# Reordering three places of a one-core audio tower kernel: additions of bo in group 0, transposes of x2 in group 1, bias rows in the last group

## The chip, the cores and the metric

One core of one Trainium2 chip. The metric is the device time of one execution in microseconds (us), over several runs; the profile is of one such execution, and its span (first to last instruction) is about 1.8 us shorter than the time. Engines: PE is TensorE's matmuls, PEld its weight loads, DVE VectorE, ACT ScalarE, POOL GpSimd, SP the sync engine. "SPq" and "ACTq" lines are DMA issues. "DMA share" is the mean busy share of the core's 16 DMA engines. "Half clock" means a stretch in which the profile's clock record grants TensorE half its speed; a "window" of it, in the recorded texts, is 3.41 us, the shorter of the two such stretches of the profile before ahead of the tail (the other has 6.83 us).

## The reference, cut to what matters

64 signals of 80,000 samples are cut into 157 frames of 512, put through an orthonormal DCT, and then through one layer:

```python
h = _L0_tok_ref(x)                                     # DCT of frames: (64, 157, 512)
h = h + _L0_attn_ref(_layernorm(h), Wk, bk, Wq, ...)   # phase attention, cumulative sums, gate
h = h + _L0_ffn_ref(_layernorm(h), Wg, bg, We, be)     # one of 16 experts for each signal

# attention, its end:
return x + total / norm @ Wo + bo
# experts:
scores = softmax(mean(x, axis=1) @ Wg + bg); idx = argmax(scores)
y = einsum('bsd,bdo->bso', x, We[idx]) + be[idx][:, None, :]
return gate * y
```

Everything is float32. The expert's matrix We[idx], 1 MB for each signal, and its bias row be[idx] can only be fetched once the router has decided.

## The kernel before: the parts that matter

The kernel works in 16 groups of four signals. A group has five "frames" of 128 tokens: four of the signals' first 128 tokens, and one (index GB = 4) that gathers the four tails of 29. While group g is in attention, group g+1 is embedded and group g-1 is in the experts. The order of the program matters on each engine: in the profile before, GpSimd runs the five additions of bo (from 44.64 us) and only then the layer norm that stands behind them (51.22).

```python
def add_bo(g, m):                     # GpSimd, 128x512
    r = S[g]["res"][m]
    nc.gpsimd.tensor_tensor(r, r, bo, ALU.add)

def phasors(g):                       # ScalarE: eight sines; then GpSimd
    ...
    nc.gpsimd.tensor_copy(by_tail(kf_t[: 2 * F]), kf[: 2 * F, :, P:L])

def turn_x2(g):                       # transposes on TensorE, each copied out by ScalarE
    for m in range(NM):
        place(s["x2T"], m, transposed(s.pop(("x2", m))), copy=copy)
        yield

for g in range(NG):
    turns = turn_x2(g - 1)
    project(g, turns if g > 1 else iter(()))   # from group 2 on, transposes between projections
    phasors(g)
    if behind:
        fold_once(g + 1, 0); fold_once(g + 1, 1); fold_twice(g + 1, 0)
        for m in range(NM):
            value(g, m)
            for _ in turns:                    # group 1: here
                pass
            if m == 0:
                route(g - 1)
                fold_twice(g + 1, 1)
                keep_value(g, m)
                route_sum(g - 1)
            elif m == 1:
                route_spread(g - 1)
            ...
    else:
        ...
        for m in range(NM):
            add_bo(0, m)                       # group 0: five at once
    for m in range(NM):
        ... embed and embed_ln of group g+1, load_frame, add_bo(g + 1, m)
        gate_part(g, m); turn(g + 1, m); scores
```

fold_once is an addition on VectorE and a subtraction on GpSimd, fold_twice two additions on VectorE; keep_value evicts a value on VectorE, that is, moves it out of the tile that TensorE wrote; route_sum reduces the router's result on VectorE and route_spread gives it back to TensorE.

The last group has no successor to hide behind. fetch asks for expert matrices (four buffers), bias for bias rows (four buffers named be, which also hold the result until its output DMA is done), add_bias adds the residual on VectorE, expert does the matmuls, the eviction and the output. The kernel follows whole; its end is the part in question.

## Time and profile before

| | before |
|---|---|
| time, median (lowest to highest) | 1566.69 us (1565.12 to 1566.76, 3 runs) |
| TensorE busy | 1538.3 us, 98% of a span of 1564.9 |
| VectorE, ScalarE, GpSimd busy | 45%, 28%, 34% |
| DMA | 135 MB, 86 GB/s in the mean |

TensorE is the bound, so I read where it stands still and what follows its last matmul. The lines are in the prediction. In the same profile's table by stretches (first column the stretch in us; the value before DMA share and GB/s is the clock granted to TensorE), two stretches show half the clock, one from shortly before the end of its longest stop (53.32) and one 1.8 us after the end of the next (112.61):

```profile
53.00:56.30 3.30, 2.98 (x13) 2.99 (x14) 0.75 (x2) 3.25 (x5) 2.23 (x4) 0.50 0.00 0
114.40:121.20 6.80, 6.13 (x39) 2.91 (x38) 0.66 (x2) 1.87 (x2) 0.72 (x1) 0.50 0.01 2
```

### The profile page before, as it was taken

To read this page: it belongs to the slowest core of one execution; us is meant where nothing else is said; L and a number is where in the kernel's file an instruction comes from. 1 tells how busy PE (TensorE), PEld (TensorE's weight loads), DVE (VectorE), ACT (ScalarE), POOL (GpSimd) and SP (SyncE) were. 2 spreads that over 40 slices of the span, in tenths; PEclk is the share of its full clock that TensorE was granted. 3 is DMA by queue.
4 is the path that set the end of the run, shared out by engine and by line. 5 is a ranking of instruction groups with operands and counts; after the bars stand their busy time and mean duration, and the time that the engine had idled before them with its cause. 6 is when DMAs were issued, how large, how long until landed. Compare 5 with 4: busy or idle time off the path is not lost.

```text
span 1564.9 us, 17536 instructions
## 1 busy us (share of the span) xinstructions
PE 1538.3 (98%) x6242; PEld 891.3 (57%) x6242; DVE 697.9 (45%) x1676; ACT 445.1 (28%) x676; POOL 529.9 (34%) x964
## 2 busy tenths in 40 slices
PE   8889999999999999999999999999999999999997
PEld 5646557465564746647465474655647456474552
DVE  4344544435444444444445443454443544444253
ACT  4332233331323314223142233313233142331210
POOL 3523423243332433323343242432324333233132
PEclk9999999999999999999999999999999999999999
DMA  5103141141311323122231311313113131222216
GB/s 182 34 0 135 41 146 49 48 141 54 137 38 47 142 61 134 34 86 103 67 134 34 133 60 57 142 48 141 41 47 141 61 134 34 72 83 65 110 36 205
DMA packets 42856, 135.26 MB, mean 86 GB/s; under 512 B 7873, under 2 KB 8401, under 8 KB 34193
## 3 DMA queue, kind: packets, MB, share of 16 engines
q0 software_dynamic: 15616, 88.09, 16.6%
q1 hardware_dynamic: 26920, 45.81, 9.0%
q8 instruction: 50, 0.82, 0.2%
q10 hardware_dynamic: 232, 0.24, 0.1%
q14 instruction: 38, 0.30, 0.1%
HBM read 113.53 MB, written 20.58 MB: 86 GB/s over the span
## 4 chain that ended last, share of the span: by engine, by line
PE 95%; DMA 2%; ACT 1%; DVE 1%; POOL 1%; issue 1%; SPq 0%; DVEq 0%; POOLq 0%
PE mm L181 48%; PE mm L401 17%; PE mm L442 9%; PE tr L162 5%; PE mm L198 4%; PE mm L590 3%; PE mm L366 2%; PE mm L196 2%; PE mm L455 2%; PE tr L495 1%; PE tr L416 1%; DMA out<-be 1%; DMA be<-in_be,expi 1%; DMA frame<-in_frames 0%; POOL res L216 0%
## 5 line engine op out<-in xcount | busy, mean ns | idle before, releaser
L401 PE MATMUL mm<-xT,wg 128*128 128x314 f32 x1024 | 281.1, 426 | 0.0
L401 PEld LDWEIGHTS mm<-xT,wg 128*128 128x128 f32 x1024 | 192.5, 188 | 72.0 <-issue 0.5
L181 PE MATMUL mm<-wv,xT 128*128 128x512 f32 x512 | 231.4, 600 | 1.7 <-ACT xT L168 1.7
L181 PE MATMUL mm<-we,x2T 128*128 128x512 f32 x512 | 223.0, 593 | 1.4 <-DMA we<-in_we,rows 1.4
L181 PE MATMUL mm<-wo,tT 128*128 128x512 f32 x512 | 222.3, 592 | 0.0
L474 ACT ACTIVATE x<-res,shift,rstd 128x512 f32<-128x512 f32 x80 | 65.1, 814 | 383.8 <-POOL shift L156 383.8
L181 PEld LDWEIGHTS mm<-we,x2T 128*128 128x128 f32 x512 | 97.0, 190 | 123.8 <-issue 120.9
L181 PEld LDWEIGHTS mm<-wo,tT 128*128 128x128 f32 x512 | 97.3, 190 | 117.2 <-issue 114.8
L153 POOL TENSOR_SCALAR rstd<-mv 128x1 f32<-128x1 f32 x160 | 42.0, 263 | 350.4 <-DVE mv L151 345.5
L181 PEld LDWEIGHTS mm<-wv,xT 128*128 128x128 f32 x512 | 94.1, 191 | 107.2 <-issue 104.5
L208 ACT ACTIVATE x<-mm,shift,rstd 128x512 f32<-128x512 f32 x80 | 62.2, 777 | 309.0 <-POOL shift L156 308.6
L442 PE MATMUL mm<-att,v 128*128 128x314 f32 x512 | 143.2, 427 | 0.0
L471 DVE TENSOR_TENSOR res<-mm,res 128x512 f32<-128x512 f32 x80 | 55.3, 692 | 150.1 <-PE mm L181 150.1
L598 DVE SCALAR_TENSOR_TENSOR be<-mm,gate,be 128x512 f32<-128x512 f32 x80 | 60.0, 751 | 118.3 <-PE mm L181 76.8
L442 PEld LDWEIGHTS mm<-att,v 128*128 128x128 f32 x512 | 94.9, 190 | 31.3
L162 PE MATMUL tr<-ident,x 128*128 128x128 f32 x640 | 94.0, 278 | 10.1 <-ACT x L208 5.1
L162 PEld LDWEIGHTS tr<-ident,x 128*128 128x128 f32 x640 | 74.0, 141 | 52.4 <-ACT x2T L168 17.7
L568 POOL DMA_INDIRECT be<-in_be,expi x80 | 82.7, 1034 | 61.0 <-issue 23.7
L430 DVE TENSOR_TENSOR tT<-mm,gT 128x314 f32<-128x314 f32 x128 | 62.3, 487 | 90.3 <-PE mm L442 84.9
L216 POOL TENSOR_TENSOR res<-res,bo 128x512 f32<-128x512 f32 x80 | 101.7, 1273 | 2.4 <-ACT res L210 2.4
L154 POOL TENSOR_TENSOR rstd<-rstd,power 128x1 f32<-128x1 f32 x160 | 96.1, 601 | 13.4
L388 POOL COPY kf_t<-kf 64x116 f32<-64x116 f32 x16 | 4.4, 278 | 271.2 <-ACT kf L385 271.2
(121 smaller groups left out, 1792.6 us busy)
## 6 DMA issues: line engine op xcount, KB each, us to landing
frame<-in_frames SPq DMA_DIRECT2D x80, 256.0 KB
out<-be SPq DMA_DIRECT2D x64, 256.0 KB
out<-be SPq DMA_DIRECT2D x60, 32.0 KB
out<-be SPq DMA_DIRECT2D x60, 26.0 KB
be<-in_be,expi POOLq DMA_INDIRECT x80
wv<-in_wv SPq DMA_DIRECT2D x1, 1024.0 KB
wg<-in_wg SPq DMA_DIRECT2D x1, 1024.0 KB
wo<-in_wo SPq DMA_DIRECT2D x1, 1024.0 KB
```

Of the source, the lines that this page charges most:

```text
L154: nc.gpsimd.tensor_tensor(rstd, rstd, power, ALU.pow)
L162: nc.tensor.transpose(tr[:, c * P : (c + 1) * P], x[:, c * P : (c + 1) * P], ident)
L181: nc.tensor.matmul(ps, lhs(c), w[:, c, :], start=(c == 0), stop=(c == C - 1))
L198: nc.tensor.matmul(by_r[:, 1::2, :], ft[:, i, :], dct_o[:, i, :], start=(i == 0), stop=(i == 1))
L208: nc.scalar.activation(x, h, AF.Identity, bias=shift, scale=rstd)
L216: nc.gpsimd.tensor_tensor(r, r, bo, ALU.add)
L401: nc.tensor.matmul(ps[:, k, : 2 * L], wg[:, c, o * P : (o + 1) * P], s["xT"][:, c, 2 * k : 2 * k + 2, :L], start=(c == 0), stop=(c == C - 1),)
L430: nc.vector.tensor_tensor(to, reads[0], th, ALU.mult)
L442: nc.tensor.matmul(ps[:, c, : 2 * L], s["v", i][:, cols], att[:, i], start=True, stop=True)
L474: nc.scalar.activation(x, r, AF.Identity, bias=shift, scale=rstd)
L568: nc.gpsimd.indirect_dma_start(out=be, out_offset=None, in_=a["be"], in_offset=bass.IndirectOffsetOnAxis(ap=s["expi"][:, m : m + 1], axis=0),)
L598: nc.vector.scalar_tensor_tensor(o, ps, s["gate"][:, m : m + 1], o, ALU.mult, ALU.add)
```

## The change

The intent: take the two stops of TensorE in the first groups away, and in the last group request bias rows without waiting for outputs to leave the buffers, and evict each frame without first adding the next frame's bias. The diff, without blank lines:

```diff
     def bias(g, m):
         s = S[g]
-        s["be", m] = be = p2.tile([P, D], F32, tag="be", name="be", bufs=4)
+        if g + 1 < NG:
+            be = p2.tile([P, D], F32, tag="be", name="be", bufs=4)
+        else:
+            be = p1.tile([P, C, P], F32, tag="frame", name="be_last", bufs=NM).rearrange("p c t -> p (c t)")
+        s["be", m] = be
...
         project(g, turns if g > 1 else iter(()))
+        if g == 1:
+            value(g, 0)
+            for _ in turns:
+                pass
         phasors(g)
...
             for m in range(NM):
-                value(g, m)
-                for _ in turns:
-                    pass
+                if m > 0 or g > 1:
+                    value(g, m)
...
             fold_twice(1, 4)
-            for m in range(NM):
-                add_bo(0, m)
...
+            if g == 0:
+                add_bo(0, m)
             if ahead:
                 add_bo(g + 1, m)
...
     pick_gate(g)
+    order = [0, 1, 2, GB, 3]
+    bias(g, order[0])
     add_bias(g - 1, ORDER[3])
     add_bias(g - 1, ORDER[4])
     expert(g - 1, ORDER[2])
-    order = [0, 1, 2, GB, 3]
-    bias(g, order[0])
     expert(g - 1, ORDER[3])
     fetch(g, [2])
     bias(g, order[1])
+    bias(g, order[2])
     expert(g - 1, ORDER[4])
     fetch(g, [3])
-    bias(g, order[2])
-    add_bias(g, order[0])
-    add_bias(g, order[1])
+    bias(g, order[3])
+    bias(g, order[4])
     for n, m in enumerate(order):
+        add_bias(g, m)
         expert(g, m)
-        if n + 3 < NM:
-            bias(g, order[n + 3])
-        if n + 2 < NM:
-            add_bias(g, order[n + 2])
```

I call the three places A (bo, group 0), B (transposes of x2, group 1) and C (last group).

## The prediction

> **What bounds the kernel now.** I read the page's busy shares and its chain of work first, then the timeline of TensorE alone to find where it stands still, then the timeline of all engines around each stop, and last DMA share and landing times in the final 40 us.
>
> ```profile
> PE 1538.3 (98%) x6242; PEld 891.3 (57%) x6242; DVE 697.9 (45%) x1676; ACT 445.1 (28%) x676; POOL 529.9 (34%) x964
> PE 95%; DMA 2%; ACT 1%; DVE 1%; POOL 1%; issue 1%; SPq 0%; DVEq 0%; POOLq 0%
> ```
>
> TensorE is busy 98% of the span and 95% of the chain. From the third group on, groups repeat every 95.28 us (values of group 3 start at 305.36, of group 2 at 210.08 in the chain in order of time) with almost no gap, so only stops of TensorE, or the tail after it, can be gained. The change touches three places; I show each.
>
> Place A, group 0, first gate stage (timeline; start, length, then the instruction):
>
> ```profile
> 44.13 4.47 PE L401 MATMUL mm<-xT,wg 128*128 128x314 f32 x16
> 44.64 6.50 POOL L216 TENSOR_TENSOR res<-res,bo 128x512 f32<-128x512 f32 x5
> ...
> 51.22 0.21 POOL L153 TENSOR_SCALAR rstd<-mv 128x1 f32<-128x1 f32 x1
> ...
> 53.32 1.12 PE L162 MATMUL tr<-ident,x 128*128 128x128 f32 x4 [4.71 <-ACT x L208]
> ...
> 57.10 4.39 PE L401 MATMUL mm<-xT,wg 128*128 128x314 f32 x16
> ```
>
> Five additions of bo sit ahead of the layer norm of group 1's first frame in GpSimd's queue; TensorE waits 4.71 us for the normalised x, and works at half speed after it.
>
> Place B, group 1, between value of frame 0 and the router:
>
> ```profile
> 107.91 0.47 ACT L384 ACTIVATE kf<-u 32x314 f32<-32x314 f32 x1
> ...
> 111.99 1.04 ACT L168 COPY x2T<-tr 128x512 f32<-128x512 f32 x2
> ...
> 112.61 1.13 PE L162 MATMUL tr<-ident,x 128*128 128x128 f32 x8 [3.57 <-ACT x2T L168]
> ...
> 115.36 2.32 PE L495 MATMUL tr<-x2T,rwg 128*32 128x157 f32 x32 [0.67 <-ACT x2T L170]
> 117.61 5.46 PE L181 MATMUL mm<-wv,xT 128*128 128x512 f32 x8
> ```
>
> Eight sines on ScalarE are ahead of the copies that empty the two transpose banks. Again a stop, then half speed: the router takes 2.32 us (1.27 at 213.45), value of frame 1 takes 5.46 (3.70 at 214.65).
>
> Place C, the last group:
>
> ```profile
> 1542.31 0.95 POOL L568 DMA_INDIRECT be<-in_be,expi  x1 [8.35 <-DMA out<-be]
> 1543.57 0.94 POOL L536 DMA_INDIRECT we<-in_we,rows  x1 [0.30 <-issue]
> ...
> 1553.06 0.95 POOL L568 DMA_INDIRECT be<-in_be,expi  x1 [5.15 <-DVE be L598]
> ```
> ```profile
> 1549.90 3.62 PE L590 MATMUL mm<-we,x2T 128*32 128x512 f32 x26 [0.77 <-DMA we<-in_we,rows]
> 1553.45 3.70 PE L181 MATMUL mm<-we,x2T 128*128 128x512 f32 x8
> ```
> ```profile
> 1557.58 0.75 DVE L579 SCALAR_TENSOR_TENSOR be<-be,gate,res 128x512 f32<-128x512 f32 x1 [3.82 <-DMA be<-in_be,expi]
> 1558.25 1.41 DVE L598 SCALAR_TENSOR_TENSOR be<-mm,gate,be 128x512 f32<-128x512 f32 x2
> 1559.03 3.60 ACTq L606 DMA_DIRECT2D out<-be  x8
> 1559.68 0.33 SPq L600 DMA_DIRECT2D out<-be  x1
> ```
>
> A bias row waits for an output to leave its buffer; the fourth expert matrix queues behind it on GpSimd. At the end the last bias row comes late, and the tails' eviction stands behind its addition on VectorE, although TensorE finished the tails at about 1553.5. Eight outputs are issued after it, the last at 1562.21; it lands at 1563.8, and the program ends 1.04 us later.
>
> [...] its clock records stand at 0.5 for 3.41 us from 52.9 and 6.83 us from 114.4, exactly after the stops of A and B. [...] additions of line 100 take 1.34 us beside the bo additions, 0.28 elsewhere. [...] an output of 256 KB takes 9.3 us beside expert matrices (1532.28 to 1541.5) and 2.2 us alone at the end.
>
> **The change, part by part.** No arithmetic is added or removed; TensorE's instruction order is identical, and only orders on ScalarE, VectorE and GpSimd, and one buffer, change.
>
> A. The five bo additions become one per step. VectorE: without them lines 100 and 101 run at 0.28, so the first statistics start at about 45.4 rather than 47.49 and end at 46.3; GpSimd's three small steps take 1.23 (51.22 to 52.45), so x is started at 47.7 and written at 48.45. The gate's matmuls end at 44.13 + 4.23 = 48.36. The stop shrinks to about 0.1. From the transposes to the next gate stage takes 2.28 us in group 1 (140.28 to 142.56), so it starts at 50.8 rather than 57.10: **6.2 us**, of which 4.6 is the stop and 1.6 the half clock. Two additions (2 x 1.27) a step plus 1.3 of statistics fit well inside a step of 6.5.
>
> B. Copies before sines. Transposes start at 108.00 as before; in group 2 the first copy starts 0.70 after the transposes, so at 108.7. From first copy to router takes 3.37 now (111.99 to 115.36), so the router starts at about 112.0, 3.3 earlier; with 1.2 for it and 3.53 for value of frame 1 TensorE is through at 116.7 rather than 122.9. But the sines now start late: copies end at 112.0, the table load takes 1.28 and four sines 2.14, so kf is complete at 115.4. In group 2, which already has this order, VectorE's router sum ends 3.25 us after the copy of kf (214.16 to 217.41), since a frame's folding on GpSimd and an eviction stand between. That gives 118.7, so the next TensorE step, spreading that sum, starts 2.0 us late, at about 118.75 against 122.91: **4.1 us**, not 6.2. I subtract 0.3 for a chance of about one in six that sparse transposes or this new stop still halve the clock (about 1.7 us for one window). Say 3.8.
>
> C. With its own buffers no bias row waits for an output. The third matrix still waits for TensorE (issued 1533.02, landed 1544.3 behind 3.25 MB; the 1.43 us stop there stays). The fourth can be requested when TensorE leaves its old buffer, about 1537 rather than 1543.57. DMA share is about 0.9 to 1.0 from 1532 to 1542, so its gain is less than those 6.5: after the third matrix (mostly landed by 1542) come two bias rows, 0.5 MB, and 1 MB; at 2.75 us per MB (landings at 226.5, 230.3, 232.7, 235.6 in group 2) that is 1546.2[...]. The tails' matmuls start at 1548.07; uninterrupted they take 3.64, now they take 5.45. TensorE thus ends about 1.8 earlier at best, 1.2 in the mean, at about 1555.9. Then the last eviction 0.75, issue, 2.16 to landing (1559.68 to 1561.84 now) and 1.04 to the end: 1555.9 + 0.1 + 0.75 + 2.16 + 1.04 = 1559.95. The tails' branch: eviction done by about 1553.2, eight issues 3.6, landing and end 2.2: 1559.0, just behind. Against 1564.9: **5.0 us**.
>
> Sum: 6.2 + 3.8 + 5.0 = 15.0 us, about 1.0%. They add, since they lie one after another on TensorE's chain. 1566.69 - 15.0 = 1551.7.
>
> **Rivals.** First: B only moves the wait. Then the new stop at the router's sum takes most of it, helped by a halved clock: B gives 1 to 2 and the total is about 1554. For it speaks that VectorE and GpSimd have a serial chain from the sines to the sum; against it that even with this chain I count 4. Second: C's matrices are bound by DMA, so the early request gains nothing on TensorE, which ends at 1557.0; only the freed eviction counts: 3.7 for C, total 1553. For it speaks DMA share near 1.0; against it the share of 0.35 in 1542 to 1544, a hole the new order fills. Third: bo additions now collide with VectorE in every step of group 0 and delay the masked scores; the slack of several us a step speaks against it. It would cost A 1 us. Fourth, upward: no half clock at all, and the fourth matrix in time: about 1550.5.
>
> **Range and chances.** A 5.5 to 6.6, B 1.5 to 4.5, C 3.5 to 6.0; runs before spread over 1.6 us[...]. Point 1551.7, range 1549.0 to 1555.5. Over 2% faster would need 31 us, twice all that is here: 1%. Over 2% slower needs an unknown failure: 1%. Within 2%: 98%.
>
> **What would show it.** A: the stop of 4.71 gone, second gate stage of group 0 near 50.8, no half clock there. B: copies ahead of the table load, router near 1.27 us, a new stop of about 2 us before the spread. C: no bias row waiting for an output; the fourth matrix requested near 1537; tails' matmuls in about 3.7 us; the tails' eviction before 1553; the last output from the sync queue last. I am wrong if the clock is still halved in group 1 for two windows, if the third matrix lands later because more requests and outputs share the engines, or if the middle groups' period moves from 95.28.

## The result, and the profile after

1551.22 us in the median (1550.40 to 1551.95, 6 runs) against 1566.03 of the kernel before in the same rounds (1564.23 to 1566.76, 6 runs). The ratio is 0.9906, with a 95% interval from 0.9894 to 0.9919. (A ratio is the mean time of one kernel's fast runs over that of the other's of the same rounds, so not quite the ratio of the medians.)

Busy shares and chain of the changed kernel:

```profile
PE 1534.1 (99%) x6242; PEld 889.2 (57%) x6242; DVE 696.5 (45%) x1676; ACT 445.0 (29%) x676; POOL 527.1 (34%) x964
PE 96%; DMA 1%; issue 1%; POOL 0%; DVE 0%; ACT 0%; SPq 0%; POOLq 0%
```

TensorE's busy time fell by 4.2 us with the same 6242 matmul records: they were not fewer, but fewer of them ran at half clock (10.24 us of it in A and B before, none there after).

Place A, timeline of all engines:

```profile
43.43 4.46 PE L401 MATMUL mm<-xT,wg 128*128 128x314 f32 x16
...
47.73 0.64 PE L162 MATMUL tr<-ident,x 128*128 128x128 f32 x4
...
48.46 2.75 POOL L216 TENSOR_TENSOR res<-res,bo 128x512 f32<-128x512 f32 x2
...
50.05 4.39 PE L401 MATMUL mm<-xT,wg 128*128 128x314 f32 x16
```

The transposes follow the gate without a stop (no bracket), the bo additions come later, two in a step, and the second gate stage starts 6.62 us after the first instead of 12.97.

Place B, the same view:

```profile
101.59 1.07 ACT L168 COPY x2T<-tr 128x512 f32<-128x512 f32 x2 [2.12 <-PE tr L162]
...
104.85 1.28 ACT L384 ACT_TABLE_LOAD   x1
104.89 1.27 PE L495 MATMUL tr<-x2T,rwg 128*32 128x157 f32 x32 [0.68 <-ACT x2T L170]
106.09 3.70 PE L181 MATMUL mm<-wv,xT 128*128 128x512 f32 x8
...
108.29 0.28 POOL L388 COPY kf_t<-kf 64x116 f32<-64x116 f32 x1 [10.08 <-ACT kf L385]
...
111.22 0.30 DVE L502 TENSOR_REDUCE tot<-tr 128x1 f32<-128x157 f32 x1
...
111.58 0.49 PE L508 MATMUL tr<-ident,tot 128*128 128x128 f32 x2 [1.79 <-DVE tot L502]
```

Copies now stand ahead of the table load, and router and value run at full speed (1.27 and 3.70). A new stop of 1.79 us has come, for the router's sum.

Place C, the same view:

```profile
1525.54 0.94 POOL L536 DMA_INDIRECT we<-in_we,rows  x1 [0.30 <-issue]
...
1537.96 3.62 PE L595 MATMUL mm<-we,x2T 128*32 128x512 f32 x26 [1.72 <-DMA we<-in_we,rows]
...
1541.62 0.75 DVE L603 SCALAR_TENSOR_TENSOR be_last<-mm,gate,be_last 128x512 f32<-128x512 f32 x1 [2.19 <-PE mm L595]
...
1542.40 3.54 ACTq L611 DMA_DIRECT2D out<-be_last  x8
...
1545.25 0.75 DVE L603 SCALAR_TENSOR_TENSOR be_last<-mm,gate,be_last 128x512 f32<-128x512 f32 x1 [2.22 <-PE mm L181]
```

No bias row waits for an output. The tails' eviction follows the tails' matmuls at once, and the last eviction follows the last matmul at once. But the fourth expert matrix, though requested 7.9 us after the group's first instead of 14.7, holds TensorE up longer than before (1.72 against 0.77 us).

The third matrix had held it up as well. Before, from the timeline of TensorE:

```profile
1544.47 3.67 PE L181 MATMUL mm<-we,x2T 128*128 128x512 f32 x8 [1.43 <-DMA we<-in_we,rows]
```

After, the page's line of the same matmuls (its last figure is their idle time, 1.4 us on the page before):

```profile
L181 PE MATMUL mm<-we,x2T 128*128 128x512 f32 x512 | 222.7, 592 | 0.0
```

So the tails began 1.66 us earlier after the group's first request (17.56 us instead of 19.22), and TensorE lost 0.95 of that again at the fourth matrix.

To add it up, I cut the profiles at fixed instructions: **stage A** from the first gate stage of group 0 to the second, **stage B** from the first transpose of x2 in group 1 to the value of frame 2, **tail** from the request of the last group's first expert matrix to the end of the span (not to be taken for the tails, the frame of the signals' last 29 tokens).

| us | stage A | stage B | tail |
|---|---|---|---|
| before | 12.97 | 15.13 | 36.01 |
| after | 6.62 | 10.95 | 31.63 |
| gain | 6.35 | 4.18 | 4.38 |

The three gains are 14.91. The spans differ by 15.6; the other 0.7 lies ahead of stage A (the first gate stage began at 43.43 and not 44.13), where nothing was changed. It began between 42.87 and 44.53 in all profiles, so I take it for chance. Between B and the tail both kernels take the same time: 1528.85 - 123.13 = 1405.72 before, 1517.62 - 111.90 = 1405.72 after.

### The profile page after: what moved, and what is told of

Same layout as the page of the kernel before. It is cut to its first block, busy times and chain, and to the rows that moved or that the text cites. A ratio compares the mean times of both kernels' runs of the same rounds, so it can differ in the third digit from the quotient of the medians.

```text
span 1549.3 us, 17525 instructions
## 1 busy us (share of the span) xinstructions
PE 1534.1 (99%) x6242; PEld 889.2 (57%) x6242; DVE 696.5 (45%) x1676; ACT 445.0 (29%) x676; POOL 527.1 (34%) x964
## 4 chain that ended last, share of the span: by engine, by line
PE 96%; DMA 1%; issue 1%; POOL 0%; DVE 0%; ACT 0%; SPq 0%; POOLq 0%
PE mm L181 48%; PE mm L401 17%; PE mm L442 9%; PE tr L162 5%; PE mm L198 4%; PE mm L595 4%; PE mm L366 2%; PE mm L196 2%; PE mm L455 2%; PE tr L495 1%; PE tr L416 1%; DMA we<-in_we,rows 1%; DMA frame<-in_frames 0%; PE tr L508 0%; PE tr L423 0%
## 5 line engine op out<-in xcount | busy, mean ns | idle before, releaser
L603 DVE SCALAR_TENSOR_TENSOR be<-mm,gate,be 128x512 f32<-128x512 f32 x75 | 56.3, 751 | 119.8 <-PE mm L181 78.2
L162 PEld LDWEIGHTS tr<-ident,x 128*128 128x128 f32 x640 | 73.7, 140 | 44.2 <-issue 14.7
L573 POOL DMA_INDIRECT be<-in_be,expi x75 | 77.2, 1029 | 45.9 <-issue 23.1
```

Of the source, the lines that this page charges most:

```text
L162: nc.tensor.transpose(tr[:, c * P : (c + 1) * P], x[:, c * P : (c + 1) * P], ident)
L573: nc.gpsimd.indirect_dma_start(out=be, out_offset=None, in_=a["be"], in_offset=bass.IndirectOffsetOnAxis(ap=s["expi"][:, m : m + 1], axis=0),)
```

## The experiments

All runs were of five rounds and gave right results. The median of the kernel before was 1565.42 in the first four, 1565.90 in the next four, 1565.08 in the last three.

**Theory:** A, B and C each act by themselves, as in the table; a part of A and B is the clock, not the stop; C is held by DMA. **Rivals:** waits only move; the parts depend on each other; within C the buffers, or the order of requests, is all that counts.

### a_only, b_only, c_only: one part at a time

The edit of each is the named part of the diff above, put into the kernel before: `add_bo` alone; `value` and `turns` ahead of `phasors` alone; the buffers and everything from `pick_gate(g)` on alone.

> Part A alone (bo of group 0 added beside the gate). My theory: the 4.71 us stop before the first transposes of the gate stage is gone and with it the half clock after it: 6.2 us off, ratio about 0.9960; the stops of group 1 and the tail stay as before. Rival (the additions now collide with VectorE in every step): a stop of 1 us or more comes back in the later gate steps, 5 us or less off.

> Part B alone (group 1's transposes of x2 and their copies ahead of the sines). My theory: the 3.57 us stop shrinks to about 0.2, a new stop of about 1.8 us comes before the spread of the router's sum, no half clock in group 1: 4.1 us off, ratio 0.9974. Rival (the wait only moves, the clock is halved all the same): 1 to 2 us off and the router at 2.3 us again.

> Part C alone (last group: bias rows in the frames' buffers, requested in another order). My theory: 4.4 us off as in the tail of the full change (ratio 0.9972), of which 0.7 from TensorE ending earlier and 3.7 from what follows its end. If the parts add up, the three single gains sum to the 15 us of the full change; rival (they overlap or depend on each other): the sum differs by over 2 us.

| | median us | off | ratio (95%) | stage A | stage B | tail |
|---|---|---|---|---|---|---|
| a_only | 1559.13 | 6.3 | 0.9960 (0.9946 to 0.9973) | 6.62 | 13.08 | 35.98 |
| b_only | 1561.87 | 3.6 | 0.9978 (0.9964 to 0.9991) | 13.13 | 10.95 | 35.38 |
| c_only | 1562.45 | 3.0 | 0.9982 (0.9968 to 0.9995) | 13.63 | 15.89 | 31.16 |

Each part does in its own stage what it does in the whole: 6.62, 10.95 and about 31.4. The medians' gains sum to 12.8, against 14.8 of the full change. Each ratio's interval is about 2 us to either side, so the sum says little: by the expectation of c_only, a sum over 2 us off would have meant that the parts depend on each other, and it is 2.0 off the measured gain and 2.2 off the forecast. It is the stages that speak against it. The profiles also show one reason why a single part can look smaller than it is: the stages that it leaves alone vary. c_only's profile holds 17.1 us of half clock in A and B, the profile before 10.2 (mean granted clock of the two runs 0.994 and 0.996), and its stages A and B are 1.4 us longer together than before's.

### a_warm: TensorE kept busy in stop A

```diff
                 gate_part(g, m)
+                if g == 0 and m == 0:
+                    warm(16)          # matmuls of the identity, result unused
```

> The kernel before with 16 idle matmuls of the identity put behind the first gate stage of group 0, so TensorE is busy for about 3.5 us of the 4.71 us stop. Theory that a part of A's gain is TensorE's clock: the wait for x still ends at the same time (53.3), but from the transposes to the next gate stage takes 2.3 us instead of 3.8, and the whole is 1.5 us faster. Rival (these matmuls are slow because what feeds them is late): 3.8 us stay and the time is unchanged.

Timeline of TensorE:

```profile
47.77 3.73 PE L143 MATMUL tr<-ident 128*128 128x128 f32 x32
52.65 0.66 PE L162 MATMUL tr<-ident,x 128*128 128x128 f32 x4 [1.15 <-ACT x L208]
...
54.99 4.39 PE L401 MATMUL mm<-xT,wg 128*128 128x314 f32 x16
```

The wait for x ends as late as before: 9.18 us after the start of the gate stage (52.65 - 43.47) against 9.19. From there to the next gate stage it takes 2.34 us instead of 3.78, and the profile has no half clock there (the four transposes take 0.66 us, 1.12 before). So 1.44 us of A is clock, and the remaining 4.9 the stop itself. The time, 1563.68 (ratio 0.9992, 0.9979 to 1.0006), agrees with 1.5 us but is too uncertain to show it; stage A, 11.52 instead of 12.97, does.

### d_fold: the new stop of B

The changed kernel, with the folding put ahead of sines and copy of kf in group 1:

```diff
             for _ in turns:
                 pass
+            fold_once(2, 0)
+            fold_once(2, 1)
+            fold_twice(2, 0)
         phasors(g)
         if behind:
-            fold_once(g + 1, 0); fold_once(g + 1, 1); fold_twice(g + 1, 0)
+            if g > 1:
+                fold_once(g + 1, 0); fold_once(g + 1, 1); fold_twice(g + 1, 0)
```

> The changed kernel with the folding of group 2's first frames put ahead of group 1's sines and of the copy of kf on GpSimd. Theory that the new stop of 1.79 us before the spread comes from the serial chain sines, copy of kf, folding, eviction, router's sum: the stop is gone, and 1.8 us are off against the changed kernel, ratio to before 0.9895. Rival (the sum waits for the router itself or the eviction): the stop stays.

```profile
106.52 3.70 PE L181 MATMUL mm<-wv,xT 128*128 128x512 f32 x8
110.06 0.39 PE L508 MATMUL tr<-ident,tot 128*128 128x128 f32 x2
110.28 7.03 PE L181 MATMUL mm<-wv,xT 128*128 128x512 f32 x16
```

The spread follows the value with no stop; stage B is 8.90 instead of 10.95. Time 1549.26, ratio 0.9892 (0.9877 to 0.9907). The cause of the new stop is settled: GpSimd's copy of kf waits for the late sines and stands ahead of the folding, and VectorE's folding stands ahead of eviction and router's sum.

### c_buffers and c_requests: the halves of C

c_buffers is the kernel before with the change of `bias` alone. c_requests is the kernel before with the new order in the last group alone, in the four old buffers.

> Of part C the frames' buffers alone, requests and additions in the old order. Theory that the waits for outputs to leave their buffers hold up the requests: the fourth matrix is requested about 6.5 us earlier, but the last additions stay ahead of the tails' eviction; since the rows are there earlier, about 3 us off, ratio 0.998. Rival (only the order of requests and additions counts): under 1 us off.

> Of part C the new order of requests and additions alone, in the old four buffers. Theory: the second row still waits for an output (up to 8 us), the fourth matrix is requested as late as before or later, and the fifth row waits for the first eviction; the tails' eviction is no longer behind the last row's addition: 1 to 3 us off. Rival (the order is all that counts): the full 4.4 us off.

| | median us | ratio (95%) | tail | fourth matrix requested, landed (after the first request) |
|---|---|---|---|---|
| before | 1565.90 | | 36.01 | 14.7, 21.0 |
| c_buffers | 1559.63 | 0.9965 (0.9951 to 0.9978) | 29.66 | 7.6, 17.8 |
| c_requests | 1565.22 | 0.9995 (0.9982 to 1.0009) | 36.73 | 16.5, 23.7 |
| both (c_only, after) | | | 31.16, 31.63 | 7.9, 19.8 to 20.3 |

(A transfer's arrival is reported in 16 parts in these traces, and I count it as landed with the last: before's third matrix was reported from 1541.94 to 1544.34, and TensorE went on at 1544.47.) Both expectations missed, in opposite directions. The buffers alone gave over 6 us in the tail, more than both together; the order alone gave nothing. In c_requests two bias rows that have to wait for their buffers stand ahead of the fourth matrix (8.03 us, which the profile puts down to an eviction, and 1.15 us, put down to an output), and TensorE waits longer in the last group than in any other kernel here (4.68 us); the 26 matmuls behind the stop take 5.32 us, 3.62 in before:

```profile
1552.24 5.32 PE L590 MATMUL mm<-we,x2T 128*32 128x512 f32 x26 [4.68 <-DMA we<-in_we,rows]
```

With the rows early, the old order of the additions does little harm: the addition just ahead of the tails' eviction waited 3.82 us for its row in before and has no wait in c_buffers. So what I had taken for a gain of the new order (evictions no longer behind a late row) was a gain of the buffers as well.

### d_fetch and ab_buffers: what the new order costs

d_fetch is the changed kernel with the fourth matrix ahead of two rows. ab_buffers is the changed kernel with the last group's old order, so with A, B and the buffers.

```diff
     fetch(g, [2])
-    bias(g, order[1])
-    bias(g, order[2])
     expert(g - 1, ORDER[4])
     fetch(g, [3])
+    bias(g, order[1])
+    bias(g, order[2])
```

> The changed kernel with the fourth expert matrix requested ahead of the second and third bias rows. Theory that the fourth matrix is held by the data queued before it: it lands 1.2 to 1.5 us earlier, the stop of 1.72 us in the tails shrinks to about 0.4, 1.3 us off against the changed kernel. Rival [...]: it lands when it did, and nothing is gained.

> The changed kernel with the last group's requests and additions put back in the old order; the frames' buffers stay. Theory from the two halves of part C: the buffers alone make the gain and the new order gives some of it back, since it puts a second bias row ahead of the fourth matrix: no stop of over 0.3 us at the tails' matmuls, 1.5 to 2 us faster than the changed kernel, ratio about 0.9895. Rival (the 2 us between the two halves' profiles were chance of the DMA): the same time as the changed kernel.

> The changed kernel once more, to stand beside the next two on one chip: ratio 0.9906, with a stop of 0.3 to 1.8 us at the tails' matmuls, where they wait for the fourth matrix.

The changed kernel once more (after_again) stood beside ab_buffers on the same chip; d_fetch had run on another.

| | median us | ratio (95%) | tail | rows ahead of the fourth matrix | fourth matrix landed |
|---|---|---|---|---|---|
| after_again | 1550.96 | 0.9907 (0.9893 to 0.9920) | 31.94 | 3 | 20.6 |
| d_fetch | 1549.92 | 0.9900 (0.9885 to 0.9915) | 29.80 | 1 | 17.3 |
| ab_buffers | 1549.69 | 0.9899 (0.9884 to 0.9914) | 29.44 | 2 | 18.0 |

(The first row is always requested early, so the new order adds one to the old.) ab_buffers, timeline:

```profile
1523.16 0.95 POOL L572 DMA_INDIRECT be_last<-in_be,expi  x1 [0.30 <-issue]
...
1525.36 0.93 POOL L536 DMA_INDIRECT we<-in_we,rows  x1 [1.25 <-PE mm L181]
1526.60 0.95 POOL L572 DMA_INDIRECT be_last<-in_be,expi  x1 [0.31 <-issue]
...
1535.64 3.76 PE L594 MATMUL mm<-we,x2T 128*32 128x512 f32 x32
```

The tails' matmuls have no stop. In the new order there was one of 0.33 to 1.84 us in four profiles (after, after_again, c_only, d_fold), where the fourth matrix landed 19.8 to 20.6 us after the first request; in the four profiles with one row fewer or the matrix first (c_buffers, ab_buffers, d_fetch, best below) it landed at 17.3 to 18.1. d_fetch's landed 3.0 us before that of the changed kernel's first profile, twice the 1.2 to 1.5 expected. The medians say 1.0 to 1.3 us, somewhat less than I expected, and the intervals of the ratios overlap, so the size in the timed runs is not sharp; the landings are. One row of 256 KB accounts for 0.7 us by my estimate, from the 2.75 us per MB of the landings in group 2. The rest is mostly the last of the matrix's 16 parts: in after it landed at 1537.9 and the fifteenth at 1536.1, while in ab_buffers the two came together. Such a lag is no property of the new order alone. In the kernel before, the third matrix's last part landed at 1544.34 and its fifteenth at 1542.63, which made the stop of 1.43 us there; d_fold has a stop of 1.22 us at the third matrix, c_only one of 0.67. With one row fewer or the matrix first, TensorE stood 0.2 us or less for third and fourth matrix together. What makes a last part lag, no run here shows.

### best: all of it together

The changed kernel with d_fold's edit, with `fetch(g, [3])` ahead of the third row (`bias(g, order[2])`), and with the tails' outputs on two queues:

```diff
-                    queue = nc.sync if g + 1 < NG else nc.scalar
+                    queue = nc.sync if g + 1 < NG or lo == 0 else nc.scalar
```

> The changed kernel with the folding ahead of group 1's sines, with the fourth matrix requested ahead of the third bias row, and with the tails' eight outputs issued by two queues in turn. If the stops were named rightly: no stop before the spread, none over 0.3 us in the tails, the span from the first request of an expert matrix to the end about 29 us rather than 31.6: 3.5 to 4.5 us faster than the changed kernel, ratio about 0.988. Rival (gains at the tail do not add): 2 us, as the folding alone.

```profile
1533.62 4.00 PE L595 MATMUL mm<-we,x2T 128*32 128x512 f32 x32
...
1537.55 3.70 PE L181 MATMUL mm<-we,x2T 128*128 128x512 f32 x8
...
1538.44 1.72 SPq L611 DMA_DIRECT2D out<-be_last  x4
1538.44 1.80 ACTq L611 DMA_DIRECT2D out<-be_last  x4
...
1542.07 0.35 SPq L605 DMA_DIRECT2D out<-be_last  x1
```

1546.87 us in the median (1546.78 to 1549.77, 4 runs), ratio 0.9886 (0.9870 to 0.9902): 4.1 us faster than the changed kernel on the same chip. Stage B is 8.90, the tail 29.29, both as expected. The eight outputs are issued in 1.8 us rather than 3.5, and the last output is again the last thing.

## Why the prediction was right

The forecast was 1551.7 us, the result 1551.22, within the range of 1549.0 to 1555.5 and within 2% as forecast. The total is closer than its parts, whose errors cancel: against one profile before and one after, A came out 0.15 above the forecast, B 0.38 above and C 0.62 below. Step by step:

- **A, forecast 6.2.** Measured 6.35 in the profiles, 6.3 alone in time. The step to the next gate stage is the 2.3 us that I had taken from group 1, so there was indeed no stop left. The split into stop and clock (4.6 and 1.6) came out as 4.9 and 1.44 (a_warm); the forecast's own lines give 1.50 for the clock (3.78 less 2.28). Over five profiles with the old order (before, b_only, c_only, c_buffers, c_requests) stage A took 12.97 to 13.64 us, so in the mean A is worth 6.6. The rival of collisions with VectorE was wrong: the longest of them, the masked addition beside two bo additions, took 0.61 us instead of 0.49, and nothing waited for it. Lines 100 and 101, 1.34 us each beside the five bo additions (44.94 and 46.22 in before), took 0.28 and 0.27 in the same place without them (44.23 and 44.44 in after); the forecast's "0.28 elsewhere" is nearly the median, 0.29 over the 80 of line 100, of which single ones take 0.80.
- **B, forecast 4.1, lowered to 3.8 for the clock.** Measured 4.18. The new stop was foreseen at 2.0 and was 1.79, on the chain that the forecast named; d_fold shows it. The clock was not halved in stage B in any of the seven profiles with the new order (five of 10.95, two of 8.90; the router took 1.27 us and the value behind it 3.70 in each), so the allowance of 0.3 was not needed; it was an estimate, one sixth of the half of 3.41 us. (The forecast read the half clock as coming "exactly after the stops"; at B it came 1.8 us after the stop had ended, 114.37 against 112.61, and at A 0.4 us before, 52.93 against 53.32.) But the size depends on what it is compared with: in six profiles with the old order stage B took between 13.08 and 15.89 us, 14.55 in the mean, since the half clock there lasted differently long: the router took 1.27 us in a_only and 2.12 to 2.32 in the other five, the value behind it 3.70 to 5.46. In the mean B is worth 3.6.
- **C, forecast 5.0.** Measured 4.38. The last stretch was right to a hundredth: from TensorE's end to the end of the span 4.05 us (1549.26 - 1545.21) as in the sum of 0.1, 0.75, 2.16 and 1.04. The mis-sized term is TensorE's earlier end: "about 1.8 earlier at best, 1.2 in the mean"; it was 0.7 (28.30 us after the first request before, 27.59 after), and it came about otherwise than forecast. The forecast kept the third matrix's stop ("the 1.43 us stop there stays") and shrank the fourth's; in the run the third's was gone and the fourth's was 0.95 longer. I had the fourth matrix landing 17.4 us after the first request by the queue alone (1546.2 on before's clock), and my mean of 1.2 allowed for a later landing, an estimate that no trace showed; fifteen of its parts were there at 18.5, the last at 20.3. (The landings quoted for 2.75 us per MB lie 2.4 to 3.8 us apart, 3.0 in the mean, so that rate was on the low side.) And I took the new order for a source of gain ("a hole the new order fills") where it was a cost: the frames' buffers alone bring the early request.
  One profile on each side is a thin base here. In four profiles with the old last group (before, a_only, b_only, a_warm) the tail took 34.53 to 36.01 us, in four with the new one (c_only, after, after_again, d_fold) 31.16 to 31.94. In the mean C is worth 3.9, of which 1.5 is TensorE's earlier end (29.02 and 27.56 us after the first request) and 2.4 what follows it; so the 1.2 was nearer than the single pair says, and the gain behind TensorE's end was put too high.
- **Rivals.** "B only moves the wait" was a part of the truth, as forecast: 1.79 us of it moved. "C's matrices are bound by DMA" was nearly right for TensorE's end: a request 6.8 us earlier brought a landing 0.7 earlier. That the fourth matrix still has something to gain from its place in the queue, c_buffers and d_fetch show.

## What to carry to other kernels

Where one engine is 98% busy, list its few stops and read for each which queue's order causes it; a wait taken away on one engine can come back (B's did, A's did not) as the next entry (1.79 us) of a serial chain on two others (here sines, copy, folding, eviction, sum), and that chain can be read beforehand from a later stage that already has the new order. A stop of the matmul engine of several us can cost more than its length (here 1.44 us of clock after a stop of 4.71), while one of 1.79 us cost none. At a tail bound by DMA (share 0.9 to 1.0 from 1532 to 1542 us before), new buffers help by letting requests go early (here the fourth matrix at 7.6 us instead of 14.7, the tail 29.66 instead of 36.01), but the order in which they go should follow the order in which the bound engine needs them: no row that VectorE needs later belongs ahead of a matrix that TensorE waits for (in the new buffers the tail took 31.16 to 31.94 with three rows ahead of the fourth matrix, 29.29 to 29.80 with one or two).

## What the clock records show

In the profile before, the clock record stands at one half for 3.41 us from 52.93 and for 6.83 us from 114.37; in the profile after it stands at full speed from 6.34 to 1549.16, of a span of 1549.26. TensorE's work in the 3.41 us ahead of a half clock, and in two more stretches of that length:

| stretch | TensorE's work | clock behind it |
|---|---|---|
| before, 49.52 to 52.93 | none | half |
| before, 107.54 to 110.96 | 1.49 us | full |
| before, 110.96 to 114.37 | 1.57 us | half |
| after, 108.74 to 112.15, with B's new stop of 1.79 us | 1.62 us | full |

So a stretch with less work was followed by full speed and one with more by half, and from these four I take no rule.
